# Neighbourhood attention in 99 steps of four key chunks instead of 168 steps of one head group, with the dense work dealt by time

## The chip, the cores and the metric

The kernel runs on one core of a Trainium2 chip. The metric is the device time of one execution in microseconds, taken as the median of several runs. The engines are named as in the profile: PE (TensorE matmuls; PEld its weight loads), DVE (VectorE), ACT (ScalarE), POOL (GpSimd) and SP (SyncE, which issues most DMAs). Each engine works through its own instructions in the order in which the program wrote them, and waits for the others by semaphores.

## The reference, cut to what matters

Two layers work on an image batch x of 2 x 56 x 56 tokens with 384 channels, in float32. The change concerns the first part of the first layer, a neighbourhood attention with 12 heads of 32 channels and a 7 x 7 neighbourhood:

```python
qkv = layer_norm(x) @ w_qkv + b_qkv            # q is scaled by 32 ** -0.5
scores = einsum('bnhwd,bnhwkd->bnhwk', q, k_nb) + bias   # k_nb: the 49 keys around a token
attn = softmax(scores, axis=-1)
out = einsum('bnhwk,bnhwkd->bnhwd', attn, v_nb)
x = x + out @ w_proj + b_proj
```

What follows (an MLP with GELU; then a second layer with a 3 x 3 depthwise convolution, four running averages over rows and columns, and another MLP) is the same in both kernels.

## The kernel before, in words

The attention goes over 14 row groups of 8 image rows (7 per image; `groups_a`, n = 0 to 13). Each group has four windows of 8 x 14 = 112 queries (j = 0 to 3 from left to right). A window's keys are the rows and columns around it, cut into chunks of at most 128 keys: two chunks where the window touches an edge of the image, three where it does not (the two inner windows of an interior group). Each window has three units, one for each group of four heads. So there are 168 units (s = 12 n + k, with k = 0 to 11 in a group), 60 of them of three chunks and 108 of two, 396 chunks in all.

For a unit, `scores` writes q times k of each chunk and head into the four PSUM banks `sc` (matmuls on 32 of PE's rows, L516); `biased` adds the position bias on DVE, in two halves of two heads (L531), and writes `pts`; `numerators` takes the exponential on ACT (L537); `gathered` adds the chunks of `pts` into `sum` on DVE (L547, L549; not in the last two groups, `END` = 12); `values` multiplies with the values `vt` into the bank `o` (L557) and sums over the keys into the bank `sums` with a matmul of ones (L564). When the three units of a window are done, ACT copies `o` to `og` (`take`, L479), DVE transposes `sums` (`gather`, L483), `invert` takes the reciprocal and widens it on POOL (L489 to L495), and `divide` transposes it back and multiplies `og` by it (L499, L501). When all four windows of a group are divided, its 128-token tiles are projected (`project`, L583) and added to the residual `xr` on DVE (L591).

Beside this the loop does the dense work of later groups on PE: query and key projections (`query_or_key`, six matmuls of 448 columns, L387), values (`value`, six of 384, L425), and the transposes of normalised x (`channels_of`, L358). The results are taken out of PSUM by ACT. DVE measures x for the layer norm of the group three ahead (`measure_x`, bn_stats; at the fourth tile it also closes the norm, L219 and L233, with a power on POOL, L222, in between).

Before, the loop has one step for each unit. A step's order is: the taking of dense pieces issued in the step before; scores for this unit, and for the next one too if both have two chunks; the values of the unit two steps back; invert or divide of an older window; measuring of x; bias and exponentials of this unit; `gathered` and `gather`; and last the step's dense pieces, one from the list `ahead` by step number and, if tiles wait in `to_project`, one projection, each in a PSUM bank of its own. The divide stands ahead of the step's bias additions:

```python
if behind is not None and hg == 0:
    behind.divide()
    if behind.j == NWC - 1:
        to_project += tiles_of(behind.n)
    ws.pop(behind.i)
```

Of the kernel before, what the change touches and what calls it, by code (L numbers as in the profile page):

```python
# [42 lines left out]
P = 128  # L43
NC = C // P
# [12 lines left out]
NWC = W // QC  # L57
NEG, BIG = -1e30, 3e38
# [115 lines left out]
def block_kernel(ctx: ExitStack, tc: tile.TileContext, ins: dict, out: bass.AP):  # L174
# [90 lines left out]
    windows = [(*s, j) for s in groups_a for j in range(NWC)]  # L265
# [17 lines left out]
    o = ps_a.tile([P, NC, TT], F32, name="o")  # L283
    sums = ps_a.tile([P, BANK], F32, name="sums")
# [3 lines left out]
    BLOCKS = -(-NC * TT // HD)  # L288
# [38 lines left out]
    load_bias(0, 0)  # L327
    load_bias(0, 1)
# [123 lines left out]
    class Window:  # L452
# [18 lines left out]
        def take(self):  # L471

            if self.n % 2 == 0 and self.j == 0:
                ogs[self.n // 2] = lp.tile([P, NC, PAIR], F32, name="og", bufs=2)
            og = ogs[self.n // 2][:, :, half_of(self.n)]
            self.og = og.rearrange("p c (r w) -> p c r w", r=QR)[
                :, :, :, self.j * QC : (self.j + 1) * QC
            ]
            nc.scalar.copy(self.og, o.rearrange("p c (r w) -> p c r w", r=QR))  # L479

        def gather(self):
            turned = lp.tile([P, BLOCKS, HD], F32, name="turned", tag="turned")
            nc.vector.transpose(turned.rearrange("p a b -> p (a b)"), sums[:, : BLOCKS * HD])  # L483
            self.totals = sm.tile([P, BLOCKS], F32, name="totals")
            nc.gpsimd.tensor_copy(self.totals, turned[:, :, 0])
# [11 lines left out]
        def divide(self):  # L497
            rec = lp.tile([P, BLOCKS * HD], F32, name="rec_t", tag="turned")
            nc.vector.transpose(rec, self.wide.rearrange("p a b -> p (a b)"))  # L499
            rec = rec[:, : NC * TT].rearrange("p (c r w) -> p c r w", c=NC, r=QR)  # L500
            nc.vector.tensor_tensor(self.og, self.og, rec, ALU.mult)  # L501


    class Unit:
        def __init__(self, w, hg):
            self.w, self.hg, self.m = w, hg, len(w.starts)

        def scores(self, first=0):

            w, hg = self.w, self.hg  # L510
            self.first = first * TT
            for c, a in enumerate(w.starts):
                r = w.r0 + a
                for i in range(4):
                    d = slice(i * HD, (i + 1) * HD)
                    nc.tensor.matmul(  # L516
                        sc[i // 2][: w.keys, i % 2, (first + c) * TT : (first + c + 1) * TT],
                        lhsT=kT[d, hg, w.keys_at + r * w.kc : w.keys_at + (r + w.rows) * w.kc],
                        rhs=qTs[w.n][d, hg, w.j, :], start=True, stop=True,
                    )  # L520

        def of(self, half):
            return self.pts[: self.w.keys, 2 * half : 2 * half + 2, : self.m, :]

        def biased(self, half):

            n, h = self.w.keys, 2 * half
            if half == 0:
                self.pts = lp.tile([P, 4, 3, TT], F32, name="pts", bufs=3)
            at = slice(self.first, self.first + self.m * TT)  # L530
            nc.vector.tensor_tensor(  # L531
                self.of(half), sc[half][:n, :, at].rearrange("p h (c q) -> p h c q", q=TT),
                self.w.bias[:n, 4 * self.hg + h : 4 * self.hg + h + 2], ALU.add,
            )

        def numerators(self, half):
            nc.scalar.activation(self.of(half), self.of(half), AF.Exp)  # L537

        def gathered(self):


            n, self.parts = self.w.keys, [self.pts[:, :, c, :] for c in range(self.m)]
            if self.w.n >= END:
                return
            t = lp.tile([P, 4, TT], F32, name="sum", bufs=2)
            self.parts = [t]
# [4 lines left out]
        def values(self):  # L551

            w, hg, n = self.w, self.hg, self.w.keys
            for c in range(self.m):
                for i in range(4):
                    h = 4 * hg + i
                    nc.tensor.matmul(  # L557
                        o[i * HD : (i + 1) * HD, hg, :],
# [3 lines left out]
            for c, part in enumerate(self.parts):  # L562
                for i in range(4):
                    nc.tensor.matmul(  # L564
                        sums[i * HD : (i + 1) * HD, hg * TT : (hg + 1) * TT], lhsT=ones_hd[:n, :],
                        rhs=part[:n, i, :], start=c == 0, stop=c == len(self.parts) - 1,
                    )

    def load_residual(t, pool=lp, bufs=3, steps=4):
# [123 lines left out]
    load_bias(0, 3)  # L693
    for t in range(3):
        load_residual(t, steps=8)
# [10 lines left out]
    units, ws, to_project, ahead, taking = {}, {}, [], [], []  # L706
    ng = len(groups_a)
    ws[0] = Window(0)


    END, THEN = ng - 2, (7, 9, 11, 13, 16, 19, 22)
    for s in range(NU + 4):
        n, k, hg, i = s // UG, s % UG, s % NC, s // NC
        if s == NU:
# [5 lines left out]
            for g in range(2):  # L720
                for t in range(T2 // P - 4 + 2 * g, T2 // P - 2 + 2 * g):
                    load_residual(t, tail_pool, 4, 2)
# [4 lines left out]
        if k == 0 and n < ng:  # L727
            vals = []
            if n + 1 < ng:
                ahead += [lambda n=n, m=m: query_or_key(n + 1, m, one_bank) for m in range(NC)]  # L730
                vals += tiles_of(n + 1)[2:]
            if n + 2 < ng:
                vals += tiles_of(n + 2)[:2]
            ahead += [lambda t=t: value(t, one_bank) for t in vals]
            if n + 2 < ng:
                ahead += [
                    lambda n=n, m=m: query_or_key(n + 2, m, one_bank) for m in range(NC, 2 * NC)
                ]

            spare = (3, 4, 5) if len(ahead) == 9 else (4, 6)  # L740
            if n == END - 1:
                spare = (3, 6, 9)

        if k == 2 and n + 4 < ng:
            load_x(n + 4)
        if k == 1 and n < ng:
            load_bias(n, NWC - 1)
        if n + 1 < ng and k in (4, 10):
            load_bias(n + 1, 0 if k == 4 else 1)
        if s == NU - UG - 4:  # L750
            ectx.close()
            wm = ctx.enter_context(tc.tile_pool(name="w_mlp", bufs=1, side="right"))
            w1, w2, w_parts = weights(0)
        if s < NU and hg == 2 and s + 1 < NU:
            ws[i + 1] = Window(i + 1)
        if s >= NU - UG - 4 and hg == 2 and w_parts:

            w_parts.pop(0)(nc.scalar)

        if s <= NU:  # L760
            for take in taking:
                take()
            taking = []
        if s == NU + 1:
            sctx.close()
            ps_s = sctx.enter_context(tc.tile_pool(name="a_pss", bufs=4, space=PSUM))
        if s < NU:

            if s not in units:
                units[s] = Unit(ws[i], hg)  # L770
                units[s].scores()
                behind = Unit(ws[(s + 1) // NC], (s + 1) % NC) if s + 1 < NU else None
                if behind is not None and (units[s].m + behind.m) * TT <= BANK:
                    behind.scores(units[s].m)
                    units[s + 1] = behind
        new, before, last = units.get(s), units.get(s - 1), units.pop(s - 2, None)
        done = last.w if last is not None and last.hg == NC - 1 else None
        if last is not None:
            last.values()
        behind = ws.get(i - 1 - (hg == 0))  # L780
        if behind is not None and hg == 2:
            behind.invert()
        if behind is not None and hg == 0:
            behind.divide()
            if behind.j == NWC - 1:
                to_project += tiles_of(behind.n)
            ws.pop(behind.i)
        if n + 3 < ng and k < NT:
            measure_x(n + 3, k)
        for half in range(2):  # L790
            if new is not None:
                new.biased(half)
                new.numerators(half)
            if half == 0 and done is not None:
                done.take()
        if before is not None:
            before.gathered()
        if done is not None:
            done.gather()
        if n < END:  # L800
            if ahead and k not in spare:
                taking.append(ahead.pop(0)())
            if to_project and n < END - 1:
                taking.append(project(to_project.pop(0), turning_bank))
        elif ahead:
            if k != 3:
                taking.append(ahead.pop(0)())
        elif s - END * UG in THEN:
            taking.append(project(to_project.pop(0), one_bank))
        elif s > NU and s < NU + 4 and to_project:  # L810
            taking.append(project(to_project.pop(0), any_bank))
        for t in list(loaded):
            loaded[t] -= 1
            if loaded[t] < 0:
                add_bias(t)
        if n + 3 < ng:
            if k in (4, 5):
                for q in range(2 * k - 8, 2 * k - 6):
                    normalize_x(n + 3, q)
            if k in (8, 9, 11):  # L820
                taking.append(channels_of(n + 3, (8, 9, 11).index(k), turning_bank))
# [1060 lines left out]
```

## Time and profile before

| | |
|---|---|
| median of 3 runs | 2632.05 us (2630.25 to 2635.82) |
| profiled execution | 2631.16 us, span of its instructions 2629.4 us |
| first and last bias addition of the attention | 49.3 and 683.2 us |
| PE, DVE, ACT busy over the whole span | 2603.2, 1987.7, 949.1 us |
| bias additions L531 | 336, mean of 448 columns 614 ns and of 672 columns 851 ns |
| exponentials L537 | 336, mean 642 ns |
| mean granted clock of PE | 0.999 |

Busy time counts the union of an engine's instructions, and the ends of matmuls are modelled, so a PE that is busy all the time may still spend part of it on changes between kinds of work; these are read from the starts of its instructions in the timeline. Idle time is put down to the instruction that released the engine.

### The profile page before, as it was taken

To read this page: it belongs to the slowest core of one execution; us is meant where nothing else is said; L and a number is where in the kernel's file an instruction comes from. 1 tells how busy PE (TensorE), PEld (TensorE's weight loads), DVE (VectorE), ACT (ScalarE), POOL (GpSimd) and SP (SyncE) were. 2 spreads that over 40 slices of the span, in tenths; PEclk is the share of its full clock that TensorE was granted. 3 is DMA by queue.
4 is the path that set the end of the run, shared out by engine and by line. 5 is a ranking of instruction groups with operands and counts; after the bars stand their busy time and mean duration, and the time that the engine had idled before them with its cause. 6 is when DMAs were issued, how large, how long until landed. Compare 5 with 4: busy or idle time off the path is not lost. (4 is left out here: it accounts for less than half of the span.)

```text
span 2629.4 us, 39158 instructions
## 1 busy us (share of the span) xinstructions
PE 2603.2 (99%) x15781; PEld 1590.3 (60%) x15782; DVE 1987.7 (76%) x3581; ACT 949.1 (36%) x1591; POOL 392.7 (15%) x404
## 2 busy tenths in 40 slices
PE   9999999999999999999999999999999999999999
PEld 5666556666655455555555555555555557888888
DVE  3878777876465688688988889889987845888871
ACT  4555555554323332223334433222233312332222
POOL 0111111110311100000010000000000042434342
PEclk9999999999999999999999999999999999999999
DMA  6432455224611123233245544633255421111000
GB/s 210 146 91 93 131 173 169 89 76 132 199 37 39 48 92 110 100 110 118 99 166 195 196 147 161 214 104 112 100 207 188 153 102 46 49 49 49 22 13 17
DMA packets 131648, 299.11 MB, mean 114 GB/s; under 512 B 10390, under 2 KB 86528, under 8 KB 129152
## 3 DMA queue, kind: packets, MB, share of 16 engines
q1 hardware_dynamic: 126512, 269.76, 29.8%
q10 hardware_dynamic: 4944, 26.74, 2.9%
q8 instruction: 126, 2.06, 0.3%
q14 instruction: 66, 0.54, 0.1%
HBM read 180.86 MB, written 115.61 MB: 113 GB/s over the span
## 5 line engine op out<-in xcount | busy, mean ns | idle before, releaser
L1091 PE MATMUL mm<-hT,w 128*128 128x512 f32 (+2 forms) x1368 | 575.0, 576 | 0.4 <-ACT hT L254 0.2
L1091 PEld LDWEIGHTS mm<-hT,w 128*128 128x128 f32 x1368 | 256.6, 190 | 286.0 <-issue 265.9
L1187 DVE SCALAR_TENSOR_TENSOR loc<-pt,taps,loc 128x990 f32<-128x990 f32 (+9 forms) x336 | 377.2, 1123 | 10.0 <-ACT loc L1169 1.7
L1102 ACT ACTIVATE hid<-mm,chan 128x512 f32<-128x512 f32 (+2 forms) x228 | 152.2, 668 | 503.4 <-PE mm L1091 503.4
L1109 PE MATMUL y_end<-w,hid 128*128 128x384 f32 x912 | 300.4, 486 | 0.0
L222 POOL TENSOR_TENSOR rs<-rs,mhalf 128x4 f32<-128x4 f32 (+4 forms) x72 | 89.2, 1239 | 1392.8 <-DVE rs L219 1357.3
L1109 PE MATMUL y<-w,hid 128*128 128x384 f32 x864 | 284.6, 486 | 0.0
L531 DVE TENSOR_TENSOR pts<-sc,bias 119x448 f32<-119x448 f32 (+3 forms) x336 | 221.0, 700 | 72.1 <-PE sc L516 69.9
L537 ACT ACTIVATE pts<-pts 119x448 f32<-119x448 f32 (+3 forms) x336 | 206.6, 642 | 183.3 <-DVE pts L531 183.2
L1109 PEld LDWEIGHTS y_end<-w,hid 128*128 128x128 f32 x912 | 172.9, 190 | 118.6
L1109 PEld LDWEIGHTS y<-w,hid 128*128 128x128 f32 x864 | 163.7, 190 | 112.3 <-issue 1.0
L387 PE MATMUL ps<-hT,wqkv 128*128 128x448 f32 x504 | 213.6, 563 | 6.1 <-ACT vs L432 4.1
L1075 DVE STREAM_TRANSPOSE hT<-xn 32x96 f32<-32x96 f32 x672 | 181.1, 269 | 37.0 <-ACT xn L240 16.4
L1091 PE MATMUL mm<-hT,w_in 128*128 128x512 f32 (+2 forms) x468 | 191.9, 569 | 0.6 <-ACT hT L254 0.6
L1091 PEld LDWEIGHTS mm<-hT,w_in 128*128 128x128 f32 x468 | 88.6, 190 | 102.0 <-issue 90.3
L387 PEld LDWEIGHTS ps<-hT,wqkv 128*128 128x128 f32 x504 | 90.7, 192 | 87.5 <-issue 73.1
L516 PEld LDWEIGHTS sc<-qT,kT 32*100 32x100 f32 (+3 forms) x3168 | 90.7, 169 | 66.7 <-issue 17.1
L1320 DVE STREAM_TRANSPOSE turned<-mx 32x192 f32<-32x192 f32 x336 | 123.9, 369 | 4.4
L240 ACT ACTIVATE xn<-xc,sh,rs 128x384 f32<-128x384 f32 x98 | 64.7, 698 | 169.6 <-DVE sh L233 169.5
L516 PE MATMUL sc<-qT,kT 32*100 32x112 f32 (+3 forms) x3168 | 113.4, 271 | 6.3 <-DVE pts L531 5.1
L557 PE MATMUL o<-pts,vt 100*32 100x112 f32 (+3 forms) x3168 | 111.1, 264 | 1.2 <-ACT og L479 1.0
L425 PE MATMUL ps<-wqkv,hT 128*128 128x384 f32 x294 | 106.9, 502 | 0.0
(168 smaller groups left out, 3627.3 us busy)
## 6 DMA issues: line engine op xcount, KB each, us to landing
loc<-loc_d SPq DMA_DIRECT2D x24, 784.0 KB
mixed<-mix_d SPq DMA_DIRECT2D x24, 784.0 KB
mix_d<-mixed SPq DMA_DIRECT2D x24, 784.0 KB
xa<-x_d SPq DMA_DIRECT2D x23, 768.0 KB
bias<-in_bias_t ACTq DMA_DIRECT2D x13, 1344.0 KB
mx<-mix_d SPq DMA_DIRECT2D x11, 1536.0 KB
p_d<-mx SPq DMA_DIRECT2D x10, 1536.0 KB
pt<-p_d SPq DMA_DIRECT2D x18, 560.0 KB
```

The costliest lines, as they stand in the source:

```text
L387: nc.tensor.matmul(ps, lhsT=wqkv[:, c, m * P : (m + 1) * P], rhs=hT[:, c, half_of(n)], start=c == 0, stop=c == NC - 1,)
L425: nc.tensor.matmul(ps, lhsT=hT[:, c, at : at + P], rhs=wqkv[:, c, 2 * C :], start=c == 0, stop=c == NC - 1,)
L516: nc.tensor.matmul(sc[i // 2][: w.keys, i % 2, (first + c) * TT : (first + c + 1) * TT], lhsT=kT[d, hg, w.keys_at + r * w.kc : w.keys_at + ...
L531: nc.vector.tensor_tensor(self.of(half), sc[half][:n, :, at].rearrange("p h (c q) -> p h c q", q=TT), self.w.bias[:n, 4 * self.hg + h : 4 ...
L537: nc.scalar.activation(self.of(half), self.of(half), AF.Exp)
L557: nc.tensor.matmul(o[i * HD : (i + 1) * HD, hg, :], lhsT=w.vt[:n, c, h * HD : (h + 1) * HD], rhs=self.pts[:n, i, c, :], start=c == 0, stop ...
L1075: nc.vector.transpose(hT[j : j + HD, :, k * P + i : k * P + i + HD], xn[i : i + HD, k, :].rearrange("p (c q) -> p c q", c=NC)[:, :, j : j ...
L1091: nc.tensor.matmul(ps[:, : n * P], lhsT=w[:, c, m * P : (m + 1) * P], rhs=hT[:, c, : n * P], start=c == 0, stop=c == NC - 1,)
L1102: nc.scalar.activation(t[:, : n * P], ps[:, : n * P], AF.Gelu, bias=col(b1, m))
L1109: nc.tensor.matmul(ps, lhsT=t[:, k * P : (k + 1) * P], rhs=w[:, m, :], start=m == 0, stop=m == len(lhs) - 1,)
L1187: nc.vector.scalar_tensor_tensor(to, pt[:, lo + dy - self.top : hi + dy - self.top, xt : xt + n], self.tap(dy, dx), to, ALU.mult, ALU.add,)
L1320: nc.vector.transpose(t[j : j + HD].rearrange("p (m c) -> p m c", m=NI)[:, :, i : i + HD], mx[i : i + HD, :, k * P + j : k * P + j + HD],)
```

## The change

The loop now runs over steps of exactly four key chunks (`CHUNKS`), whatever units they belong to; a unit may be split over two steps. 396 chunks make 99 steps, each with parts of two units. In each group the two edge columns come first (`ORDER` = 0, 3, 1, 2). A step writes the scores of its four chunks, then the values of the four chunks of the step before, then the bias additions and exponentials of its own parts. The banks `o` and `sums` become rings of four slots of 128 columns: three units of a window take three slots, and the next window's first unit the fourth; a window whose slots wrap around is copied and transposed in two pieces.

The dense pieces of a group are put in a list with an assumed time for each (2.24, 1.92 and 0.4 us). `Dense.step` deals them so that the time dealt grows evenly over the group's steps, alternating projections with other pieces as long as both are there, and the banks `one_bank` and `turning_bank` in turn; each piece is taken out of PSUM by instructions issued straight behind it. `invert` comes at the head of the step after `gather`; `divide` comes in that step behind the bias additions, `gather` and `gathered`, directly ahead of the dense pieces. The bias tables and the values `vt` are loaded at other unit numbers, `pts` and `sum` have four buffers. The diff, cut to its core:

```diff
+ORDER = (0, NWC - 1, *range(1, NWC - 1))
+CHUNKS, SLOTS = 4, 4
...
-    windows = [(*s, j) for s in groups_a for j in range(NWC)]
+    windows = [(*s, j) for s in groups_a for j in ORDER]
...
-    o = ps_a.tile([P, NC, TT], F32, name="o")
-    sums = ps_a.tile([P, BANK], F32, name="sums")
+    o = ps_a.tile([P, SLOTS, P], F32, name="o")
+    sums = ps_a.tile([P, SLOTS, P], F32, name="sums")
...
-            nc.scalar.copy(self.og, o.rearrange("p c (r w) -> p c r w", r=QR))
+            for c, at, n in self.runs():
+                nc.scalar.copy(
+                    self.og[:, c : c + n],
+                    o[:, at : at + n, :TT].rearrange("p c (r w) -> p c r w", r=QR),
+                )
+        def runs(self):
+            at = NC * self.i % SLOTS
+            n = min(NC, SLOTS - at)
+            return [(0, at, n)] + ([(n, 0, NC - n)] if n < NC else [])
         def gather(self):
             turned = lp.tile([P, BLOCKS, HD], F32, name="turned", tag="turned")
-            nc.vector.transpose(turned.rearrange("p a b -> p (a b)"), sums[:, : BLOCKS * HD])
+            for c, at, n in self.runs():
+                nc.vector.transpose(
+                    turned.rearrange("p a b -> p (a b)")[:, c * P : (c + n) * P],
+                    sums[:, at : at + n, :].rearrange("p c q -> p (c q)"),
+                )
...
+            self.slot = (NC * w.i + hg) % SLOTS
+            self.pts, self.whole = None, None
...
+        def scores(self, lo, hi, at):
             w, hg = self.w, self.hg
-            self.first = first * TT
-            for c, a in enumerate(w.starts):
-                r = w.r0 + a
+            for c in range(lo, hi):
+                r = w.r0 + w.starts[c]
+                q = (at + c - lo) * TT
                 for i in range(4):
                     d = slice(i * HD, (i + 1) * HD)
                     nc.tensor.matmul(
-                        sc[i // 2][: w.keys, i % 2, (first + c) * TT : (first + c + 1) * TT],
+                        sc[i // 2][: w.keys, i % 2, q : q + TT],
                         lhsT=kT[d, hg, w.keys_at + r * w.kc : w.keys_at + (r + w.rows) * w.kc],
                         rhs=qTs[w.n][d, hg, w.j, :], start=True, stop=True,
...
+        def biased(self, half, lo, hi, at):
             n, h = self.w.keys, 2 * half
-            if half == 0:
-                self.pts = lp.tile([P, 4, 3, TT], F32, name="pts", bufs=3)
-            at = slice(self.first, self.first + self.m * TT)
+            if self.pts is None:
+                self.pts = lp.tile([P, 4, 3, TT], F32, name="pts", bufs=4)
             nc.vector.tensor_tensor(
-                self.of(half), sc[half][:n, :, at].rearrange("p h (c q) -> p h c q", q=TT),
-                self.w.bias[:n, 4 * self.hg + h : 4 * self.hg + h + 2], ALU.add,
...
+            if self.w.n >= END:
+                whole = [(self.pts[:, :, c, :], c == 0, c == self.m - 1) for c in range(lo, hi)]
+            else:
+                whole = [(self.whole, True, True)] if hi == self.m else []
+            for part, first, final in whole:
                 for i in range(4):
                     nc.tensor.matmul(
-                        sums[i * HD : (i + 1) * HD, hg * TT : (hg + 1) * TT], lhsT=ones_hd[:n, :],
-                        rhs=part[:n, i, :], start=c == 0, stop=c == len(self.parts) - 1,
+                        sums[i * HD : (i + 1) * HD, self.slot, :TT], lhsT=ones_hd[:n, :],
+                        rhs=part[:n, i, :], start=first, stop=final,
...
+    need = [
+        len(chunks_of(spans(place(g, NG), KR, KRE), spans(place(j, NWC), KC, KCE))[0])
+        for _, g, j in windows
+    ]
+    stream = [(s, c) for s in range(NU) for c in range(need[s // NC])]
+    parts = []
+    for q in range(0, len(stream), CHUNKS):
+        part = []
+        for at, (s, c) in enumerate(stream[q : q + CHUNKS]):
+            if part and part[-1][0] == s:
+                part[-1][2] = c + 1
+            else:
+                part.append([s, c, c + 1, at])
+        parts.append(part)
+    NS = len(parts)
+    begins = [next(t for t, p in enumerate(parts) if [n * UG, 0] in [x[:2] for x in p]) for n in range(ng)]
+    begins.append(NS)
...
+    QK, VAL, TURN = 2.24, 1.92, 0.4
+    banks, turns = (one_bank, turning_bank), []
+    def next_bank():
+        turns.append(0)
+        return banks[len(turns) % 2]()
+    class Dense:
+        def __init__(self, n):
+            self.n, self.jobs, self.done, self.was = n, [], 0.0, False
+            vals = []
+            if n + 1 < ng:
+                for m in range(NC):
+                    self.jobs.append((QK, lambda m=m: query_or_key(n + 1, m, next_bank)))
+                vals += tiles_of(n + 1)[2:]
+            if n + 2 < ng:
+                vals += tiles_of(n + 2)[:2]
+            for t in vals:
+                self.jobs.append((VAL, lambda t=t: value(t, next_bank)))
+            if n + 2 < ng:
+                for m in range(NC):
+                    self.jobs.append((QK, lambda m=m: query_or_key(n + 2, NC + m, next_bank)))
+                    if n + 3 < ng:
+                        self.jobs.append((TURN, lambda c=m: channels_of(n + 3, c, next_bank)))
+            self.steps = begins[n + 1] - begins[n]
+            self.total = sum(w for w, _ in self.jobs)
+            self.total += VAL * (len(tiles_of(n - 1)) if n else 0)
+        def step(self, j):
+            due, final = self.total * (j + 1) / self.steps, j == self.steps - 1
+            while True:
+                ready = len(to_project) > (2 if self.n == ng - 1 else 0)
+                project_next = ready and not (self.jobs and (self.was or self.n == END))
+                if not project_next and not self.jobs:
+                    break
+                w = VAL if project_next else self.jobs[0][0]
+                if self.done + 0.5 * w > due and not (final and self.jobs):
+                    break
+                self.done += w
+                self.was = project_next
+                if project_next:
+                    project(to_project.pop(0), next_bank)()
+                else:
+                    self.jobs.pop(0)[1]()()
...
+        if k == 1:
+            load_bias(n, ORDER[2])
+        if n + 1 < ng and k in (4, 7):
+            load_bias(n + 1, ORDER[0 if k == 4 else 1])
+        if hg == 1 and i + 1 < len(windows):
+            ws[i + 1] = Window(i + 1)
+        if n + 3 < ng and k < NT:
+            measure_x(n + 3, k)
+        if n + 3 < ng and k in (4, 5):
+            for q in range(2 * k - 8, 2 * k - 6):
+                normalize_x(n + 3, q)
...
+    gathered, inverted = None, None
+    for t in range(NS + 2):
+        part = parts[t] if t < NS else []
+        before = parts[t - 1] if 0 < t <= NS else []
+        fresh = [s for s, lo, _, _ in part if lo == 0]
+        if t == NS:
...
+        if gathered is not None:
+            gathered.invert()
+        inverted, gathered = gathered, None
+        for s in fresh:
+            if s % UG == 0:
+                dense = Dense(s // UG)
...
+            hooks(s)
+            units[s] = Unit(ws[s // NC], s % NC)
...
+        for s, lo, hi, at in part:
+            units[s].scores(lo, hi, at)
+        if t == NS and to_project:
+            project(to_project.pop(0), next_bank)()
+        done = None
+        for s, lo, hi, _ in before:
+            units[s].values(lo, hi)
+            if hi == units[s].m:
+                u = units.pop(s)
+                if u.hg == NC - 1:
+                    assert done is None
+                    done = u.w
         for half in range(2):
-            if new is not None:
-                new.biased(half)
-                new.numerators(half)
+            for s, lo, hi, at in part:
+                units[s].biased(half, lo, hi, at)
+                units[s].numerators(half, lo, hi)
             if half == 0 and done is not None:
                 done.take()
-        if before is not None:
-            before.gathered()
         if done is not None:
             done.gather()
+        for s, lo, hi, _ in part:
+            if hi == units[s].m:
+                units[s].gathered()
+        if inverted is not None:
+            inverted.divide()
+            if inverted.i % NWC == NWC - 1:
+                to_project += tiles_of(inverted.n)
+            ws.pop(inverted.i)
+        if part:
+            dense.step(t - begins[dense.n])
+        elif t == NS + 1:
+            while len(to_project) > len(tiles_of(ng - 1)):
+                taking.append(project(to_project.pop(0), any_bank))
...
```

## The prediction

> **What bounds the kernel now.** I read the page first, for who is busy.
>
> ```profile
> PE 2603.2 (99%) x15781; PEld 1590.3 (60%) x15782; DVE 1987.7 (76%) x3581; ACT 949.1 (36%) x1591; POOL 392.7 (15%) x404
> ```
>
> PE is never long without work. The change touches only the attention, so I then asked for the stages between the first bias additions of successive row groups (columns: stretch, length, then busy time and instructions of PE, PEld, DVE, ACT, POOL, granted clock, DMA).
>
> ```profile
> 135.30:185.30 50.00, 49.99 (x675) 30.74 (x673) 39.28 (x81) 26.68 (x49) 7.60 (x13) 1.00 0.31 96
> 185.30:231.50 46.20, 46.19 (x663) 28.51 (x661) 38.64 (x81) 26.39 (x48) 6.63 (x12) 1.00 0.30 91
> 281.50:331.30 49.80, 47.93 (x663) 29.05 (x661) 38.75 (x81) 26.23 (x48) 6.63 (x12) 0.97 0.42 139
> 653.90:684.00 30.10, 26.57 (x586) 19.15 (x588) 21.82 (x52) 13.61 (x28) 7.58 (x13) 1.00 0.73 241
> ```
>
> An interior group is 46 to 50 us of PE without a gap, with DVE at 39 us beside it. Only the last three groups (568.0 to 684.0) idle: 7.6 us in all. So what PE saves counts in full, and so does every wait put into PE's queue. To price things I read the timeline of PE and DVE in one stretch each (start, duration, instruction, idle time before).
>
> ```profile
> 156.60 0.38 PE L564 MATMUL sums<-sum,ones_hd 100*32 100x112 f32 x8
> 156.91 2.20 PE L425 MATMUL ps<-wqkv,hT 128*128 128x384 f32 x6
> 158.95 2.10 PE L583 MATMUL ps<-wproj,og 128*128 128x384 f32 x6
> ...
> 161.56 0.54 DVE L499 STREAM_TRANSPOSE rec_t<-wide 128x352 f32<-128x352 f32 x1
> 162.13 0.51 DVE L501 TENSOR_TENSOR og<-og,rec_t 128x336 f32<-128x336 f32 x1
> 162.56 1.61 DVE L531 TENSOR_TENSOR pts<-sc,bias 100x672 f32<-100x672 f32 x2
> ...
> 196.65 0.16 DVE L219 SCALAR_TENSOR_TENSOR rs<-mv,ones 112x4 f32<-112x4 f32 x1
> 198.01 0.16 DVE L233 SCALAR_TENSOR_TENSOR sh<-mv,rs 112x4 f32<-112x4 f32 x1 [1.20 <-POOL rs L222]
> 198.09 1.62 DVE L531 TENSOR_TENSOR pts<-sc,bias 100x672 f32<-100x672 f32 x2
> ...
> 677.90 2.28 DVE L531 TENSOR_TENSOR pts<-sc,bias 102x448 f32<-102x448 f32 x4
> ```
>
> Read by starts: a dense piece of six matmuls takes 2.04 us when another follows (156.91 to 158.95); the divide of a window 1.00 (161.56 to 162.56); closing a measured x group holds DVE 1.44 (196.65 to 198.09), most of it waiting for POOL; four bias additions of two chunks 2.3. Last, who waits for the divide now:
>
> ```profile
> L501 DVE TENSOR_TENSOR og<-og,rec_t x56: 508/509/736, 67.9 to 688.3; 128x336 f32<-128x336 f32 x56
> ...
>   PEld ps L583: 0.7, 4
> ```
>
> The projection, which takes `og` as its weights, waits 0.7 us in the whole run.
>
> **The change part by part.**
>
> *99 steps for 168.* Matmuls of the attention stay the same in number. What goes is visits: each time PE turns from sums to a dense piece, 8 sums take 0.31 us (156.60 to 156.91) where 8 of 24 in a row take 0.20; each time it turns from a dense piece to scores, the piece takes 2.13 (201.22 to 203.35 in the timeline) instead of 2.04. Together 0.20. I count 149 such visits between 48 and 686 us, and about 97 will remain: -52 x 0.20 = **-10.4 us**, all on the path.
>
> *Idle time in the last groups.* Fuller steps fill part of the 7.6 us; the last group stays bound by the loop scores, bias, scores on DVE. I take **-4**, with 0 and -7.6 as ends.
>
> *Splitting units.* 99 steps of two parts and two halves are 396 bias additions for 336. From the means of 672 columns (851 ns) and 448 (614), a column costs 1.06 ns and an instruction 0.14 us: 60 x 0.14 = 8.4 us on DVE, under 1 us in an interior group, and transposes and copies that a ring's wrap splits in two add about 0.4. DVE then has some 40.5 us of a group's 45 to 49: beside PE, nothing. If that cover were gone it would be the 8.4 us.
>
> *Loads.* The windows' values are now asked for at the second head group, some 12 us ahead as before; the bias loads on ACT's queue have 16 us or more where the slowest in the trace took 10.6 from issue to its last packet. SP passes the same DMAs in a like order. Nothing, or up to 3 us if they meet in groups 6 to 8, where DMA is busiest.
>
> *Rings of four slots.* A window's last sums no longer hold up the next one's first: 2.3 us in all (PE waits for the copy of `o`, L479) at most. Taken as nothing.
>
> *The divide and the projection.* This is where I expect the time to go. Before, a window is divided at the head of a step, ahead of the bias additions; its group is projected at the step's end, behind other dense work. After, `divide` stands behind the step's bias additions, `gather` and `gathered`, and `dense.step` follows at once. When the window was the group's last, its tiles join `to_project` in that very call, and since `was` is still false (only jobs ran so far), the first piece dealt is a projection. By the rule of `Dense` with its own weights this holds in groups 1 to 11; group 12 puts jobs first. So PE stands with the projection's weight load until DVE has gone through its whole step, and the scores of the next step queue behind it on PE.
>
> PE's way there, from the end of the step's scores: values of four chunks 0.77 (24 matmuls, three chunks, start 0.60 apart from what follows), sums of two units 0.4, the turn 0.1: **1.3 us**. DVE's way at its shortest: bias 2.3, two units' sums 1.1 (0.53 to 0.62 each), divide 1.0: 4.4. So the wait is at least **3.1**, and longer by what DVE is late and by a `gather` (0.5) in that step. DVE is late because these are the group's first steps, which also hold the measuring of x (0.8 a tile, two tiles in a step) and its closing (1.44), in front of the bias additions.
>
> Groups that begin on a step boundary (3, 5, 9): in the step before, bias 2.3, two three-chunk units' sums 2.4, a divide 1.0 and then two measures 1.6 make 7.3, against 5.5 on PE (values and sums 1.0, dense 3.3, turns 0.2, scores 1.0): 1.8 late. Next step: 1.8 + bias 2.3 + gather 0.5 + sums 1.1 + invert 0.35 + two measures 1.6 + closing 1.44 = 9.1 against PE's 7.1 (1.2, two pieces 4.7, turns 0.2, scores 1.0): 2.0 late. In the step of the divide: 2.0 + 4.4 - 1.3 = **5.1**.
>
> Groups that begin inside a step (2, 4, 8, 10) divide one step later: bias 2.3 + gather 0.5 + sums 1.1 + invert 0.35 + measure 0.8 + closing 1.44 = 6.5 against 4.7 on PE, which is dealt one piece there: 1.8 late, and 1.8 + 4.4 + gather 0.5 - 1.3 = **5.4**.
>
> Group 1, behind an edge group, is 1.2 late: 4.3. Groups 6 and 7 are dealt more in the step before, so DVE is on time: 4.4 + 0.5 - 1.3 = 3.6 each. Group 11 measures nothing: 3.1. Sum: 3 x 5.1 + 4 x 5.4 + 4.3 + 2 x 3.6 + 3.1 = **+51.5 us**, between 11 x 3.1 = 34 and, with 1.5 more each, 68.
>
> *The clock behind such a wait.* The trace has one long wait of PE in the attention, and what came behind it:
>
> ```profile
> 316.00:319.50 3.50, 1.65 (x44) 1.11 (x39) 3.21 (x6) 1.06 (x3) 0.00 (x0) 1.00 0.58 188
> 319.50:323.00 3.50, 3.50 (x6) 1.46 (x5) 0.79 (x2) 0.98 (x3) 0.00 (x0) 0.51 0.99 323
> ...
> 318.98 4.22 PE L387 MATMUL ps<-hT,wqkv 128*128 128x448 f32 x6 [1.85 <-ACT vs L432]
> ```
>
> After 1.85 us of idling the granted clock was 0.51 for 3.4 us; idle stretches up to 1.35 us elsewhere left it alone. Half of 3.4, so 1.7 us, is lost. All eleven waits are longer than 1.85: 11 x 1.7 = **+18.7**, between 0 (the slow stretch falls into the wait itself) and 37 (two such stretches each).
>
> The Trainium skill ("TensorE: Matmul & The Clock Gate", Part 1, the two states) speaks against the change here: the array falls to half clock after at least one idle window of about 3.4 us and comes back after one busy window. By that rule the 1.85 us above should have cost nothing, and the row says otherwise; by the rule alone my waits of 3.1 and 3.6 us could go free and the sum would be some 5 us lower. I go by the row.
>
> *Sum*, on the profiled run (span 2629.4, time 2631.2, which is 0.9 under the median): 2631.2 - 10.4 - 4 + 51.5 + 18.7 = 2687.0; as a median **2688 us**.
>
> **The rivals.**
>
> *The divide is in time (faster).* One thing decides: whether PE has at least 3.1 us of other work between its sums and the first projection. If a job stands in front, or tiles of an older group are still left, the wait is gone with its clock loss, and 2631.2 - 10.4 - 4 = 2617 remains (2611 if all idle time of the last groups goes). For it: the deal is even, so two pieces a step are usual. Against it: the weights of `Dense` use up the older tiles within their group.
>
> *DVE becomes the engine that ends the steps.* With 40.5 of 45 us and its order fixed, DVE could be late in later steps as well, so that PE waits for `sum` too. For it: steps that end two three-chunk units hold 2.3 + 2.4 + 1.0 or more. Against: PE needs `sum` only behind the next scores, 7 us after. 1 us more in each of 75 steps: 2750.
>
> *It comes out even.* DVE reaches the divide early, waits come to 1.3 a group without clock loss: 14, against -14.4.
>
> **How the numbers follow.** A change under 0.2% (5 us) can't be told from none. The projection's wait: 0.74, its own range 2631.2 - 18 + 34 = 2647 to 2631.2 - 8 + 68 + 30 = 2721. Divide in time: 0.17. DVE throughout: 0.05. Even: 0.04. Faster 0.18, same 0.04, slower 0.78. For 8 in 10 the range must take in part of the fast case and may leave out the far end of the slow one: 2612 to 2714.
>
> **What would show it.** In the changed profile: the projection's weight load waits for `og` of the divide some 35 to 70 us in all, eleven times, longest 5 to 6; granted clock below 1 in the groups between 90 and 570 us; visits near 97; DVE near 515 us in the attention, 396 bias additions. If PE shows no gap there and groups last 44 and 49 us, the fast rival is right.

## The result and the profile after

The changed kernel takes 2694.93 us (median of 4 runs, 2693.49 to 2699.65), the kernel before 2632.6 in the same comparison: a ratio of 1.0239, 95% interval 1.0221 to 1.0257. The forecast was 2688 in a range of 2612 to 2714. The profiled execution took 2693.49 us, with a span of 2691.6, 62.2 longer than before.

The page first: the engines' busy time, PE's row of 40 slices and the granted clock.

```profile
PE 2603.6 (97%) x15782; PEld 1602.8 (60%) x15782; DVE 2004.6 (74%) x3669; ACT 959.6 (36%) x1679; POOL 408.7 (15%) x404
...
PE   9988999889999999999999999999999999999999
...
PEclk9998999899999999999999999999999999999999
```

PE now has slices below nine tenths in the attention, and the clock falls there too. Two groups of the same page carry the longest added wait and the split bias additions.

```profile
L605 PE MATMUL ps<-wproj,og 128*128 128x384 f32 x294 | 126.8, 578 | 63.9 <-DVE og L518 63.9
L546 DVE TENSOR_TENSOR pts<-sc,bias 119x448 f32<-119x448 f32 (+5 forms) x396 | 219.1, 616 | 88.7 <-PE sc L535 88.0
```

The same two groups in the kernel before:

```profile
L583 PE MATMUL ps<-wproj,og 128*128 128x384 f32 x294 | 105.6, 498 | 0.1
L531 DVE TENSOR_TENSOR pts<-sc,bias 119x448 f32<-119x448 f32 (+3 forms) x336 | 221.0, 700 | 72.1 <-PE sc L516 69.9 <-ACT pts L537 1.7
```

PE stood idle for 63.9 us in front of the projection's matmuls until the divide of `og`, where it was 0.1 before, and one matmul took 578 ns on average where it took 498: the half clock. The 396 bias additions are no more busy than the 336 were (219.1 against 221.0 us). The waits between 48 and 750 us say the same by who waited (total, times, longest):

```profile
DVE xr L613 <- PE ps L605: 66.1, 24, 4.4
PE ps L605 <- DVE og L518: 61.8, 12, 6.3
DVE sh L235 <- POOL rs L224: 13.8, 11, 1.5
PE ps L389 <- ACT kT L414: 7.5, 11, 1.4
```

The twelve waits of L605 are one in each of the groups 1 to 11, 59.1 us together, and one of 2.7 us in the last group. A thirteenth, of 2.2 us, ends behind this window. One of the eleven, in group 2, from the timeline of PE and of DVE:

```profile
144.85 1.10 PE L535 MATMUL sc<-qT,kT 32*119 32x112 f32 x32
146.86 0.38 PE L586 MATMUL sums<-sum,ones_hd 119*32 119x112 f32 x8
153.20 4.18 PE L605 MATMUL ps<-wproj,og 128*128 128x384 f32 x6 [5.97 <-DVE og L518]
157.17 3.00 PE L427 MATMUL ps<-wqkv,hT 128*128 128x384 f32 x6
160.11 1.07 PE L535 MATMUL sc<-qT,kT 32*119 32x112 f32 x32
...
146.22 0.16 DVE L221 SCALAR_TENSOR_TENSOR rs<-mv,ones 112x4 f32<-112x4 f32 x1
147.59 0.16 DVE L235 SCALAR_TENSOR_TENSOR sh<-mv,rs 112x4 f32<-112x4 f32 x1 [1.20 <-POOL rs L224]
147.67 2.21 DVE L546 TENSOR_TENSOR pts<-sc,bias 119x448 f32<-119x448 f32 x4
149.79 0.57 DVE L496 STREAM_TRANSPOSE turned<-sums 128x384 f32<-128x384 f32 x1
150.86 1.16 DVE L565 TENSOR_TENSOR sum<-pts 119x448 f32<-119x448 f32 x2 [0.49 <-ACT pts L556]
151.94 0.57 DVE L515 STREAM_TRANSPOSE rec_t<-wide 128x384 f32<-128x384 f32 x1
152.54 0.51 DVE L518 TENSOR_TENSOR og<-og,rec_t 128x336 f32<-128x336 f32 x1
```

PE's scores end at 145.9 and its sums at 147.2. DVE is still closing the norm of x, begins the bias additions only at 147.67, then does the gather, the sums and the divide, which ends at 153.05; PE starts the projection at 153.20. That piece takes 3.97 us from start to start and the value piece behind it 2.94, where each should take 2.04.

Where the 62 us lie: I added up PE's timeline from the first scores to the first transpose of the MLP (48.0 to 700.3 before, 45.4 to 762.2 after). Idle stretches over 0.1 us went from 13.4 to 75.9 us; the loss by half clock (half of PE's busy time in stretches of granted clock 0.5) from 1.7 to 29.1; all other time of PE from 637.2 down to 611.8. That is 62.5 + 27.4 - 25.4 = 64.5, less 2.6 by which the attention began earlier (its start lies between 44.3 and 48.8 us in the twelve profiled executions of this document, so that is not put down to the change).

### The profile page after: what moved, and what is told of

The parts are those of the page before. It is cut to its first block, busy times and chain, and to the rows that moved or that the text cites. A ratio compares the mean times of both kernels' runs of the same rounds, so it can differ in the third digit from the quotient of the medians.

```text
span 2691.6 us, 39324 instructions
## 1 busy us (share of the span) xinstructions
PE 2603.6 (97%) x15782; PEld 1602.8 (60%) x15782; DVE 2004.6 (74%) x3669; ACT 959.6 (36%) x1679; POOL 408.7 (15%) x404
## 3 DMA queue, kind: packets, MB, share of 16 engines
q8 instruction: 126, 2.06, 0.3%
## 5 line engine op out<-in xcount | busy, mean ns | idle before, releaser
L546 DVE TENSOR_TENSOR pts<-sc,bias 119x448 f32<-119x448 f32 (+5 forms) x396 | 219.1, 616 | 88.7 <-PE sc L535 88.0
L556 ACT ACTIVATE pts<-pts 119x448 f32<-119x448 f32 (+5 forms) x396 | 211.4, 574 | 169.4 <-DVE pts L546 162.7
L389 PE MATMUL ps<-hT,wqkv 128*128 128x448 f32 x504 | 205.9, 551 | 9.0 <-ACT kT L414 7.5
L605 PE MATMUL ps<-wproj,og 128*128 128x384 f32 x294 | 126.8, 578 | 63.9 <-DVE og L518 63.9
L605 PEld LDWEIGHTS ps<-wproj,og 128*128 128x128 f32 x294 | 61.5, 219 | 109.0 <-issue 78.5
```

Of the source, the lines that this page charges most:

```text
L389: nc.tensor.matmul(ps, lhsT=wqkv[:, c, m * P : (m + 1) * P], rhs=hT[:, c, half_of(n)], start=c == 0, stop=c == NC - 1,)
L546: nc.vector.tensor_tensor(self.pts[:n, h : h + 2, lo:hi, :], sc[half][:n, :, at * TT : (at + hi - lo) * TT].rearrange("p h (c q) -> p h c ...
L556: nc.scalar.activation(t, t, AF.Exp)
L605: nc.tensor.matmul(ps, lhsT=ogs[t // 7][:, c, at : at + P], rhs=wproj[:, c, :], start=c == 0, stop=c == NC - 1,)
```

## The experiments

The theory was the prediction's: PE stands in front of a group's first projection until DVE has gone through its step, and the clock falls behind the wait. The rivals are named with each run.

**The projection one step later** (e1_next_step).

```diff
-            if inverted.i % NWC == NWC - 1:
+            if inverted.i % NWC == NWC - 1 and not part:
                 to_project += tiles_of(inverted.n)
...
             dense.step(t - begins[dense.n])
+            if inverted is not None and inverted.i % NWC == NWC - 1:
+                to_project += tiles_of(inverted.n)
```

> The changed kernel, with one thing undone: a group's tiles become ready for projection one step after the divide of its last window, not in the same step. Theory (PE stands in front of the projection until DVE's divide, and the clock falls behind it): the eleven waits, 59.1 us in the changed kernel's trace, and the half-clock stretches behind them, 25.7 us of PE work, both go: 2694.9 - 59.1 - 25.7 = 2610 us (2602 to 2620), below the kernel before. Rival (DVE has too much to do in a group's first steps, wherever the wait shows): PE then waits for DVE at the scores or the sums instead, and 30 us or more of waits remain: 2640 to 2670.

Measured: 2630.52 us, ratio to before 0.9991 (0.9981 to 1.0001). The eleven waits are gone from the trace, and with them 64 us; but it is 20 us over the theory's number, between the two. PE still idles 30.6 us, where 75.9 less the eleven waits would leave 16.8, and the loss by half clock is 7.1 us. The idle time stands elsewhere: 12.7 in front of key and query pieces, 7.3 of scores, 6.4 of values. So the rival was partly right: the 7.3 are waits for DVE's bias additions, and 9.0 of the 12.7 are five waits for DVE too: it takes the projection out of the bank that the next key piece needs, but only behind its step's sums. One of them, from the timeline (a turn on the other bank lies between the two pieces):

```profile
168.20 2.20 PE L605 MATMUL ps<-wproj,og 128*128 128x384 f32 x6
170.59 1.46 DVE L567 TENSOR_TENSOR sum<-sum,pts 100x448 f32<-100x448 f32 x1
171.98 0.54 DVE L613 TENSOR_TENSOR xr<-ps,xr 128x384 f32<-128x384 f32 x1
172.57 1.77 PE L389 MATMUL ps<-hT,wqkv 128*128 128x448 f32 x4 [1.78 <-DVE xr L613]
```

The other 3.7 us are six waits of 0.61 for ACT, which takes a key piece out. The runs from e6_job_order on go after these waits.

**PE kept at work through the wait** (e2_fill_wait). Extra matmuls into the projection's bank, which it overwrites:

```diff
+        if fill:
+            for _ in range(fill.pop()):
+                nc.tensor.matmul(
+                    ps, lhsT=wproj[:, 0, :P], rhs=wproj[:, 0, :], start=True, stop=True
+                )
```

> The changed kernel with 7 extra matmuls of 384 columns (0.68 us each, 4.8 us) written to the projection's own bank, which it then overwrites, ahead of a group's first projection in groups 1 to 11. The wait for the divide stays, but PE works through most of it; the remaining idle time is under 1.85 us each. Theory (the clock's loss comes on top of the wait): most of the 25.7 us go, less some 3 us where the extra work is longer than the wait: 2672 us (2666 to 2682). Rival (the wait alone accounts for it, the half-clock stretches cost PE nothing that matters): 2694 to 2699.

Measured: 2676.07 us, ratio 1.0166 (1.0152 to 1.018). The timeline of PE around the same wait:

```profile
146.03 4.78 PE L607 MATMUL ps<-wproj 128*128 128x384 f32 x14
151.95 2.20 PE L612 MATMUL ps<-wproj,og 128*128 128x384 f32 x6 [1.14 <-DVE og L518]
153.99 2.10 PE L427 MATMUL ps<-wqkv,hT 128*128 128x384 f32 x6
156.02 1.07 PE L535 MATMUL sc<-qT,kT 32*119 32x112 f32 x32
```

The divide still ends as late, but the projection takes 2.04 us again (151.95 to 153.99). There is no half-clock stretch in groups 1 to 11. In the profiled executions the loss by half clock fell from 29.1 to 6.8 us, while the extra matmuls took 1.8 us more than the idle time that they filled. So some 19 to 22 us of the slowdown are the clock, against a rival of none.

**The divide ahead of the bias additions** (e3_divide_first).

```diff
+        if inverted is not None:
+            inverted.divide()
         for half in range(2):
             for s, lo, hi, at in part:
                 units[s].biased(half, lo, hi, at)
...
         if inverted is not None:
-            inverted.divide()
```

> The changed kernel with the divide moved ahead of the step's bias additions on DVE; the first projection stays in the same step. Theory (the length of the wait is what stands ahead of the divide on DVE): each wait loses bias additions (2.2) and sums (1.1) and, where there is one, the gather (0.5): eight waits of about 2.5, the others under 1, 22 us in all, with half-clock stretches left in those eight: 2694.9 - 59 + 22 - 26 + 16 = 2648 us (2630 to 2660). Rival (what counts is DVE's whole work in these steps, not the order): 2685 to 2697.

Measured: 2629.57 us, ratio 0.9992 (0.9981 to 1.0004); 18 better than the theory said. PE's idle time in front of projections fell from 63.9 to 14.9 us. In groups 1 to 11 the waits come to 13.1, where I had said 22, the longest is 1.95, and only that one has a half-clock stretch behind it; I had put one behind each of eight. The order on DVE makes the wait; both terms were over-estimated here, the clock's more, since the waits of 1.5 to 1.7 us left it alone.

**The order alone, in the kernel before** (e4_before_late_divide). The divide moved behind the sums, and the projection issued ahead of the other dense piece:

```diff
-        if behind is not None and hg == 0:
-            behind.divide()
-            if behind.j == NWC - 1:
-                to_project += tiles_of(behind.n)
-            ws.pop(behind.i)
...
             done.gather()
+        if behind is not None and hg == 0:
+            behind.divide()
+            if behind.j == NWC - 1:
+                to_project += tiles_of(behind.n)
+            ws.pop(behind.i)
         if n < END:
-            if ahead and k not in spare:
-                taking.append(ahead.pop(0)())
             if to_project and n < END - 1:
                 taking.append(project(to_project.pop(0), turning_bank))
+            if ahead and k not in spare:
+                taking.append(ahead.pop(0)())
```

> The kernel before with only the order changed: the divide moved behind the step's bias additions and sums, and the projection issued ahead of the other dense piece. Theory (the order alone makes the wait, 99 steps or not): in ten groups DVE reaches the end of the divide 2.7 us after PE reaches the projection (bias 1.5, sums 0.5, divide 1.0 and 0.3 of lateness, less values and sums 0.7): 27 us, and up to 17 us of half clock behind them: 2632.6 + 27 + 17 = 2677 us (2655 to 2682). Rival (the wait needs the fuller steps of the change): 2632 to 2642.

Measured: 2666.1 us, ratio 1.0124 (1.0108 to 1.014). Its waits, and the timeline of DVE and PE in one of them:

```profile
PE ps L583 <- DVE og L501: 25.2, 10, 2.7
...
152.30 0.37 PE L564 MATMUL sums<-sum,ones_hd 119*32 119x112 f32 x8
154.77 0.51 DVE L501 TENSOR_TENSOR og<-og,rec_t 128x336 f32<-128x336 f32 x1
155.33 3.38 PE L583 MATMUL ps<-wproj,og 128*128 128x384 f32 x6 [2.66 <-DVE og L501]
```

Ten waits of 2.1 to 2.7 us, and half-clock stretches that cost PE 13.7 us. Order by itself, on DVE and on PE, makes a kernel slower that has none of the other parts of the change.

**Measuring x later** (e5_measure_later). In the changed kernel, to see where DVE's lateness comes from:

```diff
-        if n + 3 < ng and k < NT:
-            measure_x(n + 3, k)
-        if n + 3 < ng and k in (4, 5):
-            for q in range(2 * k - 8, 2 * k - 6):
+        if n + 3 < ng and 4 <= k < 4 + NT:
+            measure_x(n + 3, k - 4)
+        if n + 3 < ng and k == 8:
+            for q in range(NT):
                 normalize_x(n + 3, q)
```

> The changed kernel with the measuring and normalising of x moved from a group's units 0 to 5 to its units 4 to 8, out of the steps ahead of the projection's wait; all else stays. Theory (2 us of each long wait are DVE's lateness, and the lateness is the measuring and its closing): the waits of groups 1 to 5 and 8 to 10 fall to about 4, those of 6, 7 and 11 stay: 16 us less, and some 4 us less of half clock: 2675 us (2665 to 2684). Rival (lateness comes from elsewhere, or the same work delays the later steps as much): 2688 to 2698.

Measured: 2675.22 us, ratio 1.0158 (1.0138 to 1.0178). All eleven waits are now between 3.41 and 3.77 us, 39.6 in all instead of 59.1: what is left is DVE's own step of bias additions, sums and divide, with the `gather` where the wait is 3.75. The wait of group 7 fell too, from 4.96 to 3.76.

**What kept e1_next_step from 2610.** First the order of a group's last pieces (e6_job_order):

```diff
-                    self.jobs.append((QK, lambda m=m: query_or_key(n + 2, NC + m, next_bank)))
-                    if n + 3 < ng:
-                        self.jobs.append((TURN, lambda c=m: channels_of(n + 3, c, next_bank)))
+                self.jobs += keys[:2] + turned[:2] + keys[2:] + turned[2:]
```

> The kernel of e1_next_step with another order of a group's last pieces: key, key, turn, turn, key, turn instead of key and turn by turns. Theory (a turn of 0.48 us between two longer pieces is too short to cover the taking of the bank that the next piece gets, which is what PE's 12.7 us in front of key projections are): they fall to about 3, 2621 us (2616 to 2626). Rival (these waits hide others of the same length): 2629 to 2633.

Measured: 2632.9 us, ratio 1.0004 (0.9993 to 1.0016): the theory of this run failed. The rival's number came true, though no hidden wait came up: the idle time in front of key and query pieces itself grew, from 12.7 to 19.3 us. The timeline of PE and ACT shows why:

```profile
78.64 0.98 PE L360 MATMUL ps<-ident,xg 112*128 112x112 f32 x8
79.56 1.05 ACT L556 ACTIVATE pts<-pts 120x448 f32<-120x448 f32 x2
80.50 1.34 ACT L365 ACTIVATE hT<-ps,chan 128x448 f32<-128x448 f32 x2
81.28 2.52 PE L389 MATMUL ps<-hT,wqkv 128*128 128x448 f32 x6 [1.66 <-ACT hT L365]
```

The two turns now come first in the step, and the bank for the third piece is emptied by ACT only behind the step's exponentials. The wait is not for the taking itself but for ACT's place in its order.

Second, the loads (e7_windows_first). In e1_next_step PE idles 5.77 us in the last group until values land, with half clock behind it; on SP's queue the window's loads stood behind a residual load that waits for a store:

```diff
-        while load:
-            load_residual(load.pop(0))
         if gathered is not None:
...
             units[s] = Unit(ws[s // NC], s % NC)
+        while load:
+            load_residual(load.pop(0))
```

> The kernel of e1_next_step with the residual's load put behind the window's value loads on SP's queue. Theory (in the last groups the window loads stand behind a residual load that waits for a store to land, which is PE's wait of 5.8 us for vt): that wait and the half clock behind it go, 8 us: 2623 us (2618 to 2628). Rival (the loads are late since DMA is full of weights at that time): 2629 to 2633.

Measured: 2618.94 us, ratio 0.9949 (0.9934 to 0.9963). The wait is gone, 11.6 us, somewhat more than said; in the profiled executions 6.0 us of it are idle time and 3.7 half clock. Three edits together did not add up (e8_all: the edits of e6_job_order, e7_windows_first and e3_divide_first on e1_next_step):

> The kernel of e1_next_step with three edits together: the order of the last pieces of e6_job_order, the loads of e7_windows_first, and the divide ahead of the bias additions as in e3_divide_first. By the theories of these, with no wait for the divide left: 2631 - 10 - 8 - 5 (scores and clock where the divide held DVE up) = 2608 us (2600 to 2616), 0.9% below the kernel before. By their rivals: 2625 to 2633.

Measured: 2641.68 us, ratio 1.0034 (1.0022 to 1.0046), neither theory. In its profiled execution, which at 2630.92 was the fastest of twelve, PE idles 24.8 us in front of key and query pieces, up to 2.98 at a time: with the job order of e6_job_order, whatever delays ACT is paid by the third piece. Most of the other 11 us of its usual execution are the clock: the profiled execution has a mean granted clock of 0.997, the eight of 2640 us and more have 0.991 to 0.995, and 0.001 of the clock over this span is 2.6 us. Why the same kernel meets more half clock in one execution than in another, no run shows.

Third, two key pieces ahead of the turn, by dealing the second key and the turn as one piece (e10_key_key_turn, on e7_windows_first):

```diff
+                    self.jobs += [
+                        (QK, key(0)), (QK + TURN, key_and_turn(1, 0)), (TURN, turn(1)),
+                        (QK, key(2)), (TURN, turn(2)),
+                    ]
```

> The kernel of e7_windows_first with a group's last pieces as key, key and turn, then turn, key, turn. In e6_job_order two turns came first in a step, and the third piece waited for a bank that ACT empties only behind the step's exponentials. Theory (a bank is free in time when a key piece of 2.4 us lies between): the 12.7 us in front of key pieces fall to about 3: 2610 us (2606 to 2614). Rival (as in e6_job_order, the wait moves to the next piece): 2617 to 2623.

Measured: 2607.25 us, ratio 0.9905 (0.989 to 0.992). The idle time in front of key and query pieces is 1.7 us, and all of PE's idle time in the attention 13.6, about as before the change. This version beats the kernel before by 1% and the changed one by 3.3%. Its stretch from first scores to MLP, beside that of the kernel before and of the changed one (length, then busy time of PE, PEld, DVE, ACT, POOL, clock, DMA), in the order before, changed, e10_key_key_turn:

```profile
48.00:700.30 652.30, 638.27 (x9061) 394.44 (x9061) 496.29 (x1038) 341.24 (x626) 98.14 (x173) 1.00 0.40 130
```

```profile
45.40:762.20 716.80, 640.84 (x9061) 408.84 (x9061) 513.17 (x1126) 351.43 (x714) 114.00 (x173) 0.95 0.36 118
```

```profile
45.40:675.60 630.20, 617.23 (x9061) 399.25 (x9060) 512.28 (x1123) 349.73 (x714) 111.31 (x173) 0.99 0.41 135
```

**The price of a visit** (e9_more_visits, on e7_windows_first). One piece between a step's scores and its values:

```diff
+        if part and len(dense.jobs) > 2 and not to_project:
+            w, job = dense.jobs.pop(0)
+            dense.done += w
+            between = job()
...
+        if between is not None:
+            between()
         if part:
             dense.step(t - begins[dense.n])
```

> The kernel of e7_windows_first with one dense piece moved between a step's scores and its values, in the steps where no projection waits and more than two pieces are left: some 48 more turns of PE to dense work and back, the same work. Theory (the prediction's price, 0.20 us a visit): 9.6 us more, 2629 us (2625 to 2632). Rival (the 25 us of PE work by which the changed kernel is shorter are all due to its 52 fewer visits, 0.45 each): 21.6 us more, 2641 us (2636 to 2646).

Measured: 2631.67 us, 12.7 over e7_windows_first, with 132 visits instead of 96, so 36 more and not 48. PE's work outside idle time and half clock went from 614.9 to 622.8: 7.9 / 36 = 0.22 a visit, close to the theory's 0.20. By the time it is more: 12.7 / 36 = 0.35 between the medians, which come from two separate comparisons, and 9.1 / 36 = 0.25 between the profiled executions. The rival's 0.45 is not reached by any of these, but the price is known only as 0.2 to 0.35.

## Why the prediction was right, and where its terms were off

- *The divide and the projection*: right in mechanism and place, and 13% low in size. The eleven waits were 4.4, 6.0, 6.3, 6.2, 6.0, 3.8, 5.0, 5.9, 6.0, 6.3 and 3.4 us, 59.1 for the 51.5 worked out; a group's first projection waits in groups 1 to 11 and not in 12. The shortest wait was said as 3.1, or 3.6 with a `gather`; with the measuring moved away (e5_measure_later) it is 3.4 and 3.75. The part for DVE's lateness was said as about 2 us in seven groups and 1.2 in one, some 14 us; moving the measuring took 19.5 us off. The surplus in the long waits is partly ACT: at 150.86 above, DVE's sums waited 0.49 us for exponentials, since ACT itself was held up by the normalising of x. That wait was not in the walk. Group 7, at 5.0 instead of 3.6, had 1.2 us of lateness that went with the measuring; the walk had put it at nothing there.
- *The clock*: 18.7 said, 27.4 found, 25.7 of it behind the eleven waits. The nine waits of 4.4 us and more were each followed by two or three slow stretches of 3.4 us, not one, and part of these fell into the wait; the one of 3.8 was followed by one, that of 3.4 by none. Filling the waits took 19 us off the time.
- *Visits*: -10.4 said. 151 visits became 96, 55 fewer instead of 52, at 0.22 by PE's work about -12 (at 0.35, -19); PE's work fell by 25.4. The rest may lie in waits too short to be told from matmuls whose ends are modelled (sums blocks alone, from start to start, fell from 58.4 to 47.4); no run separates it.
- *Idle time in the last groups*: -4 said, and the sign was wrong. In groups 11 to 13 PE idled 8.2 us before and, without the wait of group 11 counted above, 9.3 after. All of the 9.3 lies in the last group, 4.9 of it in the two further waits of a projection for the divide, which the forecast did not have.
- *Splitting units*: nothing was forecast. DVE's busy time in the attention rose to 513 us (515 forecast) beside PE; no run takes the splitting away by itself.
- *Loads*: "nothing, or up to 3 us" was wrong by its place. In the changed kernel PE waited 0.6 us for values in the last group; with the waits for the divide gone it was 5.8, and the loads' order was worth 11.6 us.
- *Missed altogether*: the dense pieces share two banks in turn, so a short piece between two long ones makes PE wait until the bank is emptied: for ACT 0.61 us once a group in the changed kernel (7.5 us in all), and in e1_next_step also for DVE. The prediction priced none of it.
- *The fast rival's price*, 2617 with the wait gone: e1_next_step gave 2630.5, since mainly for these last two reasons PE idles 17 us more than in the kernel before and loses 5 more by half clock. With both mended it is 2607 (e10_key_key_turn), below that price: its idle time is about that of before (13.6 against 13.4), and PE's work is 25 us less instead of the 10.4 said. The 2611 given beside that price is a slip (2631.2 - 10.4 - 7.6 is 2613), and so is 2750 for DVE as the engine that ends the steps: 75 us on the sum would be 2762.
- *The sum*: 2688 against 2694.9 is in part luck. The eleven waits, the last groups and the clock came out some 21 us above the forecast, and PE's work 15 us below it.

## What to carry to other kernels

Before moving an operation within a step, write down for each engine what now stands ahead of it and who stops for it: here one in-order engine's whole step was put in front of the weights of the busiest engine's next piece. Price such a wait with the clock behind it, and remember that it hides others: when it goes, the next late transfer or bank shows. A thing dealt "by time" on one engine needs its inputs a step earlier, and a short piece doesn't cover the emptying of a bank by an engine with its own queue.

## What the runs showed of the hardware

The half clock comes in stretches of 3.413 us or multiples of it, and in each run all of them start on one grid of 3.413 us: in the changed kernel at 94.13, 152.16, 206.77 and 261.38 us, 17, 16 and 16 steps apart. What counts is how much of PE's idle time falls into one step of the grid. In the attention of the twelve profiled executions, each of the 37 steps at full clock in which PE idled 1.96 us or more had half clock in the next step; of 80 with 1.18 to 1.96 us 21 had; of 2130 with less, none. (PE's idle time is read with modelled ends, and what decides between 1.18 and 1.96 no run shows.)

So the length of a wait alone does not tell what follows. Of PE's idle stretches, those up to 1.6 us were not followed by half clock when they stood alone; of eleven between 1.65 and 1.86 us (e6_job_order) two were; of ten between 2.06 and 2.66 (e4_before_late_divide) eight. In the changed kernel ten of eleven between 3.4 and 6.3 were, most of them by 6.8 or 10.2 us; the 3.42 of group 11 lay with 1.70 and 1.71 in two steps and had none. In e1_next_step two idle stretches of 0.82 and 0.60 us, 0.47 apart, had one behind them in two of three groups; there all but 0.06 us of both lay in one step, and in the third a step ended at 482.35, near the end of the first of the two. Short waits in one step count together. In the changed kernel's half clock a projection of six matmuls took 3.97 us instead of 2.04.
